# A four-layer graph network on one core: both halves of layer 0's rows in one step, and the last two output transfers moved to another queue

## The chip, the cores and the metric

The kernel runs on one core of a Trainium2 chip. The metric is the device time of one execution in microseconds, and smaller is better. A core has five engines with a queue each: TensorE (PE, matrix products; PEld is its weight load), VectorE (DVE), ScalarE (ACT), GpSimd (POOL) and SyncE (SP). Each works through its own queue in order. An instruction that has to wait holds everything behind it in that queue. SP and ACT also issue the DMA transfers here.

## The reference, cut to what matters

The input is `x` (4096 rows of 64) and a 0/1 matrix `adj` (4096 x 4096, float32, 67 MB). Four layers run one after the other, each as

```
x = layernorm(x + layer(x, adj, weights))
```

- Layer 0: `deg = sum of adj's row + 1`; `h = (adj @ x + x) / deg`; `z = relu([x, h] @ W + b)`; the result is `z / max(norm(z), 1e-12)` by rows.
- Layers 1 and 3 (hyperbolic attention): for each pair (i, j) a weight `sigmoid(left_i + right_j + b) * adj_ij` and a local vector `logmap(x_i, x_j)`; the weighted sum over j goes through `expmap` and a projection, which is row work: long chains of small operations on 8 numbers per partition.
- Layer 2: each row takes its last 100 neighbours with weights that halve from one to the next, times `x @ weight`, plus a bias.

## The kernel before, in words

**Tiling.** The 4096 rows of the result are four groups of 1024, in the order 3, 2, 1, 0 (`GROUPS`). A group has 8 blocks of 128 rows (`blocks(s)`). `adj` is read once in each layer for each group: 16 loads of 1 MB (`load`, L696 to L700), two blocks of 128 columns each, also from the last to the first. That makes 256 loads, all issued on SP, into six buffers (`f_loads`). A load can be issued only when its buffer is free again.

**Pairs and rows.** In every layer two kinds of work are interleaved. The *pairs* work through the loaded 1 MB pieces. In layer 0 (L1392 to L1440) they are eight bf16 products for each piece (L1408). In layers 1 and 3 (`attend`, L1025 to L1089) each block has six products into a `z` tile (L1059, L1062, L1065), a sigmoid and a square on ACT (L1074, L1077), two fused operations on DVE (L1080, L1082) and the products into `acc` (L1037). The *rows* are the work on a finished group: `end_0`, `norm_rows` and `prepare` after layer 0, `move` after layers 1 and 3. They are written as generators; each `yield n` asks to be continued n ticks later.

**What sets the order.** `later(steps, second)` puts a generator into one of two hand-made queues. `tick(n)` (L614 to L627), called by the pairs, continues the generator at the head of each of the two, queue 0 first. `near()` is 3 ticks in layer 0 and 1 in layers 1 to 3. Layer 0 has four ticks for each loaded piece. In layers 0 and 2 the order of the instructions of PE and ACT is the written order (`manual_schedule`); elsewhere, and on DVE, POOL and SP throughout, the compiler orders the ready instructions by its own estimates when the program is built. The order of each queue is then fixed.

**PSUM for row work.** Row work takes a PSUM buffer with `take` (L667 to L674). There is one, `aux`. While the list `spare` is not empty, a second is used in turn; in layer 0 it is `aux_2` (L1308 to L1310). `held` has an entry for each buffer taken; `free()` (L681 to L683) lets a step wait until `held` is empty, whichever queue it is in. `spare_ends()` (L676 to L679), called at the end of layer 0 (L1442), waits until `held` is empty and clears `spare`. The tiles of layer 1 (`p_sb`, L1446) are laid into the memory that layer 0's pools leave.

**`end_0` (L1357 to L1390)** makes the rows of a group from its sums, in two halves of four blocks. A half waits with `free()`, takes a buffer, makes eight pairs of float32 products (L1365, L1366), and takes them on DVE: a reciprocal of the degree (L1369), a multiplication (L1371) and the addition of `xw` (L1373). The first half ends with `yield near()`. Then come `relu` (L1376), the squares on POOL (L1378), the sum and root (L1380 to L1382), `norm_rows` and `prepare`. `prepare` queues its second part in queue 1: among other things four sets of transposes (L943) into a taken buffer, with a copy by ACT (L947). The last group's `end_0` is queued just before `spare_ends()`, so its steps run during the first ticks of layer 1.

**The end.** In layer 3 each group's new rows are written by `move` (L1098 to L1219) and sent out by `store` (L1611 to L1613), one transfer of 256 KB for each group, issued on ACT. `move` works on POOL for groups 3, 2 and 1 and on DVE for the last, group 0. It begins with two pairs of products (L1126), each copied by ACT (L1128). `attention` (L1452 to L1470) queues the store of a group while the next one's pairs run or behind them: the store of group 1 is queued when the pairs of group 0 are over, beside the `move` of group 0. After the stores the program reads a flag, `n_fit`, on every engine (L1652) and branches (L1653) over a general fallback that is not run here.

Of the kernel before, what the change touches and what calls it, by code (L numbers as in the profile page):

```python
# [10 lines left out]
F32 = mybir.dt.float32  # L11
# [8 lines left out]
P = 128  # L20
N = 4096
D = 64
# [3 lines left out]
SB = W // P  # L26
# [5 lines left out]
WB = WW // P  # L32
# [26 lines left out]
def gnn_stack_kernel(  # L59
# [15 lines left out]
    nc = tc.nc  # L75
    V = nc.vector
# [492 lines left out]
    def stream(fits):  # L569

        with ExitStack() as st:
# [19 lines left out]
            queues, place, done, held = ([], []), [0, 0], set(), []  # L591
# [65 lines left out]
            def near():  # L657

                return 3 if place[0] == 0 else 1
# [5 lines left out]
            spare, turn_of = [], [0]  # L665

            def take(dtype, *shape):  # L667


                held.append(1)  # L670
                turn_of[0] += 1
                if not spare or turn_of[0] % 2:
                    return aux.tile(list(shape), dtype, name="aux")
                return spare[0](dtype, shape)  # L674
# [6 lines left out]
            def free():  # L681
                while held:
                    yield 1  # L683
# [3 lines left out]
            def x_of(layer):  # L687

                if layer not in layers_x:
                    layers_x[layer] = xs.tile([P, NB, D], F32, name="x")  # L690
                return layers_x[layer]

            def blocks(s):
                return slice(s * WB, (s + 1) * WB)
# [7 lines left out]
            def grp(name, bufs=None):  # L702
                kw = {"bufs": bufs} if bufs else {}
                return row.tile([P, WB, D], F32, name=name, **kw)

            def nums(name, n=WB):
                return row.tile([P, n], F32, name=name)

            def over(v):
                return v[:, :, None].to_broadcast([P, v.shape[1], D])  # L710

            def rsqrt(a, name):

                n = a.shape[1]
                r, t = nums(name, n), nums("rs_t", n)
                V.tensor_scalar(
                    r.bitcast(I32), a.bitcast(I32), -0.5, float(0x5F3759DF), ALU.mult, ALU.add
                )
                for _ in range(3):
                    V.tensor_mul(t, r, r)  # L720
                    V.scalar_tensor_tensor(t, t, -0.5, a, ALU.mult, ALU.mult)
                    V.scalar_tensor_tensor(r, t, 1.5, r, ALU.add, ALU.mult)
                return r
# [138 lines left out]
            def norm_rows(layer, s, v, x2_to):  # L862

                m, v2, sq = nums("n_m"), nums("n_v2"), grp("sq")
                V.tensor_reduce(m, v, AX.X, ALU.add)
                V.tensor_scalar(m, m, 1.0 / D, None, ALU.mult)
                yield soon()
                V.tensor_sub(v, v, over(m))  # L868
                nc.gpsimd.tensor_mul(sq, v, v)  # L869
                yield soon()  # L870
                yield soon()
                V.tensor_reduce(v2, sq, AX.X, ALU.add)
                yield soon()
                V.tensor_scalar(m, v2, 1.0 / D, 1e-5, ALU.mult, ALU.add)
                r = rsqrt(m, "n_r")
                yield soon()
                V.tensor_mul(x_of(layer)[:, blocks(s), :], v, over(r))
                V.tensor_mul(x2_to, r, r)
                V.tensor_mul(x2_to, x2_to, v2)
                yield soon()  # L880
# [366 lines left out]
            def supports(s):  # L1247
# [40 lines left out]
                out=enter, in_=pass_by, compare_op=ALU.is_gt, fill=0.0, base=0,  # L1288
# [14 lines left out]
            with ExitStack() as lp:  # L1303
# [10 lines left out]
                xw = own.tile([P, NB, D], F32, name="xw")  # L1314
                sum_w = own.tile([P, D + 1], F32, name="sum_w")
                count_w = own.tile([D + 1, D + 1], F32, name="count_w")
# [39 lines left out]

                def end_0(s, tops):  # L1357
                    z = grp("z0")
                    for h, (top, low) in enumerate(tops):
                        yield from free()  # L1360
                        t = take(F32, P, SB, P)
                        for k in range(SB):
                            cols = slice(k * P, (k + 1) * P)
                            to = t[:, k, : D + 1]
                            nc.tensor.matmul(to, top[:, cols], sum_w, start=True, stop=False)  # L1365
                            nc.tensor.matmul(to, low[:, cols], count_w, start=False, stop=True)  # L1366
                        at = slice(s * WB + h * SB, s * WB + (h + 1) * SB)
                        d = nums("deg", SB)
                        V.reciprocal(d, t[:, :, D])  # L1369
                        zz = z[:, h * SB : (h + 1) * SB, :]  # L1370
                        V.tensor_mul(zz, t[:, :, :D], over(d))  # L1371
                        held.pop()
                        V.tensor_add(zz, zz, xw[:, at, :])  # L1373
                        if h == 0:
                            yield near()
                    V.tensor_scalar(z, z, 0.0, None, ALU.max)  # L1376
                    sq, n2 = grp("sq"), nums("n2")
                    nc.gpsimd.tensor_mul(sq, z, z)  # L1378
                    yield 1
                    V.tensor_reduce(n2, sq, AX.X, ALU.add)  # L1380
                    V.tensor_scalar(n2, n2, 1e-24, None, ALU.max)
                    n = rsqrt(n2, "n")  # L1382
                    yield 1
                    V.tensor_mul(z, z, over(n))
                    V.tensor_add(z, z, x0[:, blocks(s), :])
                    yield 1
                    yield from norm_rows(1, s, z, x2[:, blocks(s)])
                    yield from prepare(
                        1, s, att1, batt1_sb, curve1, 1e-15, good[:, 0], 70
                    )  # L1390

                with tc.manual_schedule(engines=FIXED):  # L1392
                    for s in GROUPS:
# [3 lines left out]
                        for g in reversed(range(NB // 2)):  # L1397
# [5 lines left out]
                            for k in (1, 0):  # L1403
                                j = 2 * g + k
                                for lhs, accs, m in parts:
                                    for h in range(2):
                                        at = k * WW + h * W
                                        nc.tensor.matmul(  # L1408
                                            accs[h][:m], lhs[:, j, :], edge[:, at : at + W],
                                            start=j == BLOCKS[0], stop=j == BLOCKS[-1],  # L1410
                                        )
                            if g == s * WB // 2 + 1:

                                for lhs, accs, m in parts:
                                    for h in range(2):
                                        for k in range(SB):
# [3 lines left out]
                                                start=False, stop=False,  # L1420
# [9 lines left out]
                        tops = []  # L1430
                        for h in range(2):
                            top = sb.tile([P, W], F32, name="top")
                            nc.scalar.copy(top, sums[h])
                            low = sb.tile([D + 1, W], F32, name="low")
                            nc.scalar.copy(low, counts[h][: D + 1])
                            tops.append((top, low))
                        later(end_0(s, tops))
                        if s > 0:
                            own_of = linear(0, s - 1, w0_sb[:D, :], own_part)
# [169 lines left out]
            place[0] = 3  # L1609

            def store(s):  # L1611
                nc.scalar.dma_start(out[:, blocks(s), :], x_of(4)[:, blocks(s), :])
                yield 1  # L1613

            attention(3, curve3, (4, 1, 1, 1), store)


            V.tensor_reduce(fits, odd, AX.X, ALU.add)
            V.tensor_scalar(fits, fits, 0.0, None, ALU.is_equal)
            t, g = nums("m1", 1), nums("g1", 1)  # L1620
# [26 lines left out]
    with tc.tile_pool(name="fit_ps", bufs=1, space=PSUM) as ps:  # L1647
        t = ps.tile([1, P], F32, name="fit_t")
# [52 lines left out]
```

## Time and profile before

| What | Value |
|---|---|
| Median of 3 runs (range) | 1115.99 us (1114.72 to 1119.29) |
| The profiled execution's own time | 1117.97 us |
| Its span, first to last instruction | 1116.2 us |
| Mean granted TensorE clock | 0.961 of full |
| Layer 0 and its seam, about | 0 to 200 us |
| Layers 1, 2 and 3, about | to 560, 800 and 1084 us |
| Last group's row work and end | 1084 to 1116.2 us |
| HBM read | 269.58 MB, 242 GB/s over the span |

How to read it. A line of the timeline gives the start in us, the duration in us, the engine, the line of the kernel, the operation, its output and input by name with shapes, and in brackets how long the engine was idle before it and what ended that idle time. ACTq and SPq are the sequencers of these engines; an issue of a DMA is such a line. A line of the chain gives start, duration, and what the time belonged to: the chain is followed back from the last instruction, at each step to what released it. A line of the windows gives a stretch of time, then for each of PE, PEld, DVE, ACT and POOL its busy us and, in brackets, how many instructions began in it, then the granted clock, the mean busy share of the 16 DMA engines and GB/s.

### The profile page before, as it was taken

What the parts mean: (1) busy time and instruction counts of PE and PEld (TensorE: products, weight loads), DVE (VectorE), ACT (ScalarE), POOL (GpSimd) and SP (SyncE); (2) the same over time, 40 slices, a digit from 0 to 9 for tenths busy, and PEclk for the clock granted to TensorE, in tenths of its full rate; (3) what the DMA queues carried; (4) which work ended last, traced back from release to release, by engine and by line L of the source; (5) the groups of instructions that cost most, each with busy time, mean ns of one, the idle gap of its engine ahead of it and who ended that gap; (6) DMA issues with size and microseconds to landing.
All of it is one profiled execution on the core that took longest, in us unless ns stands there. A gap on an engine that the chain in (4) does not pass through costs nothing.

```text
span 1116.2 us, 13744 instructions
## 1 busy us (share of the span) xinstructions
PE 996.4 (89%) x4861; PEld 393.9 (35%) x4949; DVE 912.1 (82%) x1452; ACT 803.4 (72%) x892; POOL 271.0 (24%) x649
## 2 busy tenths in 40 slices
PE   4998889789999999998998997788899999999960
PEld 2455455233333333332333332223333333333320
DVE  5677977999999999999366476447989999999965
ACT  0013122989999999896776788889899999998940
POOL 0011210010144443424500010000001544345281
PEclk8899999899999999999999999899899999999995
DMA  8899999546576576663987986587456766666300
GB/s 339 346 422 376 366 423 382 204 136 243 195 238 219 184 244 217 218 210 130 360 306 275 370 277 228 203 276 252 166 194 221 247 215 216 238 224 224 126 1 23
DMA packets 38581, 271.63 MB, mean 243 GB/s; under 512 B 4710, under 2 KB 4710, under 8 KB 5734
## 3 DMA queue, kind: packets, MB, share of 16 engines
q1 hardware_dynamic: 37440, 269.50, 66.4%
q10 hardware_dynamic: 1062, 1.15, 0.3%
q8 instruction: 41, 0.67, 0.2%
q14 instruction: 38, 0.31, 0.1%
HBM read 269.58 MB, written 1.05 MB: 242 GB/s over the span
## 4 chain that ended last, share of the span: by engine, by line
PE 58%; DVE 22%; ACT 9%; POOL 4%; DMA 4%; issue 3%; ACTq 0%; SPq 0%; POOLq 0%; DVEq 0%
PE acc L1037 14%; PE z L1563 9%; DVE t L1082 8%; DVE t L1080 6%; PE z L1062 6%; PE acc L1408 6%; PE z L1059 6%; PE z L1065 6%; PE acc L1575 3%; DMA edges<-in_adj_dram 3%; ACT sq L1077 3%; ACT sq L1570 3%; ACT sig L1074 2%; PE z L1575 1%; PE aux L943 1%
## 5 line engine op out<-in xcount | busy, mean ns | idle before, releaser
L1080 DVE SCALAR_TENSOR_TENSOR t<-z,sig 128x1024 f32<-128x1024 f32 x256 | 308.9, 1218 | 13.8 <-ACT sq L1077 7.7
L1077 ACT ACTIVATE sq<-z,turn 128x1024 f32<-128x1024 f32 x256 | 278.1, 1112 | 46.2 <-PE z L1065 17.8
L1082 DVE SCALAR_TENSOR_TENSOR t<-sq,t 128x2048 f32<-128x2048 f32 x128 | 297.4, 2323 | 0.5
L1074 ACT ACTIVATE sig<-left_b,right 128x1024 f32<-128x1024 f32 x256 | 286.2, 1147 | 1.8 <-DVE t L1080 1.3
L1037 PE MATMUL acc<-t,xe 128*64 128x512 f32 x1024 | 255.6, 611 | 18.4 <-DVE t L1082 17.9
L1062 PE MATMUL z<-lo_hi,hi_lo 128*128 128x512 f16 x512 | 194.6, 380 | 3.8 <-issue 1.0
L1065 PE MATMUL z<-dst,src 74*128 74x512 f16 x512 | 195.6, 382 | 0.0
L1059 PE MATMUL z<-edges,two_i 128*128 128x512 bf16 x462 | 181.5, 393 | 8.1 <-DVE t L1080 8.1
L1570 ACT ACTIVATE sq<-z,at_edge 128x512 bf16<-128x512 f32 (+1 forms) x192 | 149.4, 829 | 44.4 <-PE z L1563 41.3
L838 DVE SCALAR_TENSOR_TENSOR t<-edges 128x2048 bf16<-128x2048 f32 x32 | 73.0, 2288 | 52.8 <-DMA edges<-in_adj_dram 52.8
L1037 PEld LDWEIGHTS acc<-t,xe 128*64 128x64 f32 x1024 | 63.8, 137 | 147.5 <-issue 83.6
L1563 PE MATMUL z<-edges,pass_by 128*128 128x512 bf16 x241 | 87.6, 400 | 18.4 <-ACT sq L1570 17.6
L1059 PEld LDWEIGHTS <-two_i 128*128 128x128 bf16 x512 | 50.2, 98 | 127.5 <-issue 82.8
L1408 PE MATMUL acc<-edges,first 128*128 128x512 bf16 x241 | 78.0, 400 | 16.1 <-DMA edges<-in_adj_dram 15.5
L1563 PE MATMUL z<-edges,enter 128*128 128x512 bf16 x240 | 85.0, 397 | 0.5
L1408 PE MATMUL acc<-edges,third 128*65 128x512 bf16 x256 | 81.4, 400 | 0.9 <-issue 0.4
L838 DVE SCALAR_TENSOR_TENSOR junk<-edges 128x2048 bf16<-128x2048 f32 x32 | 73.1, 2286 | 4.6 <-DMA edges<-in_adj_dram 4.3
L1065 PEld LDWEIGHTS <-src 74*128 74x128 f16 x512 | 49.3, 96 | 70.5 <-issue 8.4
L1062 PEld LDWEIGHTS <-hi_lo 128*128 128x128 f16 x512 | 50.4, 98 | 58.0 <-issue 12.5
L1575 PE MATMUL acc<-sq,halves 128*64 128x512 bf16 x384 | 61.6, 398 | 2.6 <-issue 1.6
L869 POOL TENSOR_TENSOR sq<-z 128x512 f32<-128x512 f32 x8 | 14.1, 1759 | 162.2 <-DVE z L868 139.5
L1133 POOL TENSOR_TENSOR w_att<-x,u 128x512 f32<-128x512 f32 x6 | 15.6, 2599 | 142.9 <-ACT u L1128 142.9
(375 smaller groups left out, 939.4 us busy)
## 6 DMA issues: line engine op xcount, KB each, us to landing
edges<-in_adj_dram SPq DMA_DIRECT2D x256, 1024.0 KB, 5.0
x<-in_x_dram SPq DMA_DIRECT2D x4, 256.0 KB
out_dram<-x ACTq DMA_DIRECT2D x4, 256.0 KB
w_sb<-in_L_gnn_W_dram ACTq DMA_DIRECT2D x1, 32.0 KB, 5.9
w_twice<-in_L_gnn_weight_dram ACTq DMA_DIRECT2D x2, 16.0 KB, 8.2
given<-in_L_gnn_b_dram ACTq DMA_DIRECT2D x1, 0.2 KB
given<-in_L_gnn_bias_dram ACTq DMA_DIRECT2D x1, 0.2 KB
given<-in_L_gnn_b_att_dram ACTq DMA_DIRECT2D x1, 0.0 KB
```

The costliest lines, as they stand in the source:

```text
L838: V.scalar_tensor_tensor(junk, a, 0.0, a, ALU.not_equal, ALU.not_equal, accum_out=odd[:, n : n + 1])
L1037: it = nc.tensor.matmul(acc[h * D : (h + 1) * D, :], xe[:, j, :], t[:, k, h * W : (h + 1) * W], start=j == BLOCKS[0], stop=j == BLOCKS[-1],)
L1059: nc.tensor.matmul(half, two_i, edge[:, at : at + W], start=True, stop=False)
L1062: nc.tensor.matmul(half, hi_lo[:, of], lo_hi[:, to], start=False, stop=False)
L1065: last = nc.tensor.matmul(half, src[:, of], dst[:, to], start=False, stop=True)
L1074: nc.scalar.activation(sig, left_b, AF.Sigmoid, bias=right[:, j : j + 1])
L1077: nc.scalar.activation(sq[:, k], zp, AF.Square, bias=turn, scale=-1.0 / UNIT)
L1080: V.scalar_tensor_tensor(t[:, k], zp, 0.0, sig, ALU.max, ALU.mult)
L1082: V.scalar_tensor_tensor(t, sq, HIGH**2, t, ALU.add, ALU.mult)
L1408: nc.tensor.matmul(accs[h][:m], lhs[:, j, :], edge[:, at : at + W], start=j == BLOCKS[0], stop=j == BLOCKS[-1],)
L1563: nc.tensor.matmul(z[:, h : h + W], lhs, rhs[:, h : h + W], start=j == BLOCKS[0], stop=True, skip_group_check=True,)
L1570: nc.scalar.activation(w, z[:, :n], AF.Exp, bias=at_edge, scale=-LN2)
```

## The change

It has two parts. In `end_0`, one `free()` stands ahead of both halves. Where `spare` is not empty, the products of both halves are made first, into two buffers, and then both are taken on DVE, with no tick between. Where it is empty, the halves go one after the other with `yield near()` between them as before, but `held` keeps its entries until both are taken, so that no other step gets a buffer in between. In `store`, the transfers of groups 1 and 0 are issued on SP and those of groups 3 and 2 on ACT as before.

```diff
--- before.py
+++ after.py
@@ -1356,23 +1356,29 @@
 
                 def end_0(s, tops):
                     z = grp("z0")
-                    for h, (top, low) in enumerate(tops):
-                        yield from free()
-                        t = take(F32, P, SB, P)
-                        for k in range(SB):
-                            cols = slice(k * P, (k + 1) * P)
-                            to = t[:, k, : D + 1]
-                            nc.tensor.matmul(to, top[:, cols], sum_w, start=True, stop=False)
-                            nc.tensor.matmul(to, low[:, cols], count_w, start=False, stop=True)
-                        at = slice(s * WB + h * SB, s * WB + (h + 1) * SB)
-                        d = nums("deg", SB)
-                        V.reciprocal(d, t[:, :, D])
-                        zz = z[:, h * SB : (h + 1) * SB, :]
-                        V.tensor_mul(zz, t[:, :, :D], over(d))
-                        held.pop()
-                        V.tensor_add(zz, zz, xw[:, at, :])
-                        if h == 0:
+                    yield from free()
+
+                    for some in ((0, 1),) if spare else ((0,), (1,)):
+                        ts = []
+                        for h in some:
+                            top, low = tops[h]
+                            t = take(F32, P, SB, P)
+                            for k in range(SB):
+                                cols = slice(k * P, (k + 1) * P)
+                                to = t[:, k, : D + 1]
+                                nc.tensor.matmul(to, top[:, cols], sum_w, start=True, stop=False)
+                                nc.tensor.matmul(to, low[:, cols], count_w, start=False, stop=True)
+                            ts.append((h, t))
+                        for h, t in ts:
+                            at = slice(s * WB + h * SB, s * WB + (h + 1) * SB)
+                            d = nums("deg", SB)
+                            V.reciprocal(d, t[:, :, D])
+                            zz = z[:, h * SB : (h + 1) * SB, :]
+                            V.tensor_mul(zz, t[:, :, :D], over(d))
+                            V.tensor_add(zz, zz, xw[:, at, :])
+                        if some == (0,):
                             yield near()
+                    held.clear()
                     V.tensor_scalar(z, z, 0.0, None, ALU.max)
                     sq, n2 = grp("sq"), nums("n2")
                     nc.gpsimd.tensor_mul(sq, z, z)
@@ -1609,7 +1615,9 @@
             place[0] = 3
 
             def store(s):
-                nc.scalar.dma_start(out[:, blocks(s), :], x_of(4)[:, blocks(s), :])
+
+                queue = nc.sync if s <= 1 else nc.scalar
+                queue.dma_start(out[:, blocks(s), :], x_of(4)[:, blocks(s), :])
                 yield 1
 
             attention(3, curve3, (4, 1, 1, 1), store)
```

## The prediction

> **What bounds the kernel now.** I read the page first (busy shares and the summary of the chain), then the chain in order of time over its two ends that the change touches, then the ACT timeline there, then all engines at the seam between layer 0 and layer 1, and last the windows of layer 0.
>
> The page: no engine is the bound throughout.
>
> ```profile
> PE 996.4 (89%) x4861; PEld 393.9 (35%) x4949; DVE 912.1 (82%) x1452; ACT 803.4 (72%) x892; POOL 271.0 (24%) x649
> PE 58%; DVE 22%; ACT 9%; POOL 4%; DMA 4%; issue 3%; ACTq 0%; SPq 0%; POOLq 0%; DVEq 0%
> ```
>
> The reader is to see POOL with 4% of the chain though it is the idlest engine, so somewhere the end waits for it. The ACT timeline of the last 33 us shows where:
>
> ```profile
> 1083.04 0.59 ACT L1088 COPY sums<-acc 128x512 f32<-128x512 f32 x1 [9.56 <-PE acc L1037]
> 1092.12 0.34 ACTq L1612 DMA_DIRECT2D out_dram<-x  x1
> 1092.50 0.38 ACT L1128 COPY ys<-aux 128x260 f32<-128x260 f32 x1 [8.88 <-POOL x L1218]
> 1094.26 0.38 ACT L1128 COPY ys<-aux 128x260 f32<-128x260 f32 x1 [1.38 <-PE aux L1126]
> 1094.67 0.63 ACT L1134 ACTIVATE xw<-ys 128x512 f32<-128x512 f32 x1
> 1100.79 0.21 ACT L1164 ACTIVATE th<-un 128x8 f32<-128x8 f32 x1 [5.49 <-DVE un L1158]
> 1111.58 0.34 ACTq L1612 DMA_DIRECT2D out_dram<-x  x1
> ```
>
> The store of group 1 (1092.12) stands on ACT's queue ahead of the first copy of the last group's `move`. The store needs group 1's rows from POOL; the copy (L1128) needs only four PE products that ran at 1083.68 for 0.71 us. ACT stood 8.88 us. The chain confirms that this wait decides the end:
>
> ```profile
> 1090.91 1.19 POOL x L1218
> 1092.12 0.34 ACTq L1612
> 1092.50 0.39 ACT ys L1128
> 1092.93 1.25 PE aux L1126 x4
> 1094.26 0.39 ACT ys L1128
> ```
>
> The other place is the seam, where layer 1's first tiles lie in the memory that layer 0 leaves:
>
> ```profile
> 188.97 0.18 DVE L1369 RECIPROCAL deg<-aux 128x4 f32<-128x4 f32 x1 [1.92 <-PE aux L1366]
> 191.22 1.06 PE L943 MATMUL aux<-ident,ys 128*128 128x128 f16 x8
> 192.31 1.01 ACT L947 COPY lo_hi<-aux 128x1024 f16<-128x1024 f16 x1 [4.24 <-PE aux L943]
> 195.44 0.18 DVE L1369 RECIPROCAL deg<-aux 128x4 f32<-128x4 f32 x1 [5.37 <-PE aux L1366]
> 196.69 1.28 ACT L1074 ACT_TABLE_LOAD   x1 [3.37 <-DVE z L1373]
> 203.03 0.59 PE L1059 MATMUL z<-edges,two_i 128*128 128x512 bf16 x1 [5.77 <-DVE t L1080]
> ```
>
> Group 0's halves are taken at 188.97 and 195.44. Between them the single aux buffer went to group 1's `lo_hi` transposes. The first sigmoid (ACT L1074) waited 3.37 us for the second half's last add (L1373, done 196.53), and PE then stood 5.77 us. Layer 0 itself runs at the transfers' rate (columns: PE, PEld, DVE, ACT, POOL busy; clock; DMA share; GB/s):
>
> ```profile
> 70.00:83.00 13.00, 12.90 (x77) 7.49 (x79) 10.82 (x34) 0.58 (x1) 2.95 (x1) 1.00 1.01 421
> 83.00:96.00 13.00, 10.35 (x45) 4.61 (x45) 12.83 (x42) 1.66 (x3) 2.86 (x7) 1.00 0.86 321
> ```
>
> **What the Trainium skill says.** "DMA: Bandwidth & Descriptors", Anatomy of one DMA: DMA engines do not wait on semaphores; the wait is held by the issuing sequencer before dispatch. The trace agrees: 8.88 us. The same page, Issuing engines are not separate DMA queues: a transfer runs on the same 16 engines whichever engine issues it. The trace agrees as to the issue: 327 to 328 ns on SP (L698), 338 to 377 on ACT (L1612). "GPSIMD Engine Reference", Specifications: GpSimd shares its SBUF interfaces with VectorE and contends with instructions with two SBUF inputs. The trace agrees: POOL's L1218 takes 1.18 us in the tail with DVE idle, 3.11 at most beside DVE. "TensorE: Matmul & The Clock Gate", Part 1: the clock falls to half after an idle window. The trace agrees: a granted 0.52 and 0.50 in 199 to 205 us, where PE stood.
>
> **The change, part by part.** *Stores on SP.* The copy can start as soon as its products are there: 1083.68 + 0.71 = 1084.39, and 0.1 for the hand-over (1094.16 to 1094.26 at the second copy), so 1084.49 instead of 1092.50: **-8.0 us**. From there to 1111.58 all is one chain of the last group (copy, PE, copy, DVE), which shifts whole. POOL's work on group 1 (1084.6 to 1092.1) now lies beside it. A DVE product of this size beside POOL took 1.08 (L1133 at 570.99) against 0.69 alone: +0.4. The smaller steps (0.17 each) may stretch over some 3.3 us while POOL runs its three wide ones; the least is 0, the most a doubling, +1.6. I take +0.3 for both: **-7.7**, bounds -8.0 and -6.0. POOL's own chain, stretched by its ratio 3.11/1.18 on its three wide operations (3.3 us in all), adds at most 5.4 us and ends at 1097.5; the last group ends near 1103.6, so group 1's store does not become the end.
>
> What SP's wait holds up: the last of the 256 loads (L698) was issued at 1043.2, so no load is behind it. Behind it are the last store and the read of n_fit (0.47 + 0.19 + 0.03 + 0.05 us: load, register operations, assertion, branch). Before, SP did these at 1096.8 in the shade; now they follow the last store. Their cover is that store's landing: issued until 1111.92, the next semaphore step on DVE at 1114.7, so 2.8 us against some 0.9. Cost 0; without the cover +1.0. The issue moves from 0.34 on ACT to 0.33 on SP: 0. Stores of groups 3 and 2 (938.2, 1028.8) stay.
>
> *Both halves of layer 0's rows.* The number of instructions is the same: 8 times 16 products, 8 reciprocals, 8 multiplications, 8 additions. What goes is one waiting step of three ticks and a wait for a free buffer in each group. For groups 3, 2 and 1 a second buffer stands in `spare`, so both halves go out together; their later row steps move up by three or four ticks, about one pair of blocks, 2.7 us (43 us for 16). Does the stage gain? It moves bytes at a share near 1.0 in most windows, so an earlier row step only changes where the dips lie (0.86 in 83 to 96). The five dips to 0.86, 0.90, 0.94, 0.98 and 0.93 of 13 us each are worth 5.1 us together: if half vanish, -2.5; if half as much is added, +2.5. I take **0**, since moving does not remove DVE work that delays the checks (L838), which free buffers.
>
> Group 0 is different: `spare` is emptied before its rows are made, so it still goes one half at a time, but the buffer is no longer offered to the other queue between the halves. The second half needs only aux back from DVE: 189.18 + 0.42 = 189.60. If PE takes it at once, it starts at 189.7 instead of 193.4: -3.7. If it stands behind the six products of the first z, it starts when `lo_hi` did, 191.2: -2.2; part of that is given back while PE's clock is low there (0.62 in 190 to 193). If PE's order puts it behind both z, nothing is gained: 0. What is late next is the row chain L1376 to L1384, which shifts with it, and the table load of 1.28. I take **-2.0**, bounds -4.0 (some of the half clock gone too) and 0. It carries to the end because PE, DVE and ACT alternate on the chain through layers 1 to 3, with no DMA wait of weight after layer 0.
>
> Sum: -7.7 - 2.0 + 0 = -9.7. The profiled execution took 1117.97 (span 1116.2, 1.8 around it), so 1108.3 on its own scale. It is 2.0 over the median of the runs, 1115.99; on that scale the forecast is **1106.3**.
>
> **Rivals.** (A, likeliest) both as above: 1106.3, its own range 1104 to 1107.5. (B) The row part gives nothing, because PE's order keeps the second half behind both z, or a later wait takes it back; only the tail counts: 1108.3. For it: the order is fixed at build from estimates, and three of four groups are DMA-bound. Against: the wait for L1373 is plain in the trace. (C) The seam gives its full 4 and layer 0's dips half vanish: 1115.99 - 7.7 - 4 - 2.5 = 1101.8. (D) The tail's wait is replaced: group 1's few DVE steps, or POOL beside DVE, hold the last group, and 5 of the 8 return: 1106.3 + 5 = 1111.3. For it: one DVE step (L754 at 1084.82) still stands between; against: it is done before the copy would be. (E, other side) In layer 0 the row steps, now one pair earlier, go ahead of the DVE checks, edge buffers come free later and loads are issued later. The gain of 9.7 turns into a loss of 0.5% when layer 0 loses over 15.3 us: its 130 us of windows at a mean share near 0.97 would have to fall to about 0.86, each as bad as the worst now. With 17 us lost: 1123. Against: six edge buffers, and no row work is added. That the change does not do what it says holds in part, for group 0, and is counted.
>
> **How the numbers follow.** Chances: A 0.45, B 0.25, C 0.14, D 0.11, E 0.05. About 0.5% (5.6 us) is what a measurement of this kernel can tell from no change: faster means under 1110.4. A, B and C lie there whole, D mostly in "same": faster 0.85, same 0.10, slower 0.05. The range takes in A, B, C with the bounds of the unknown costs (-8.0 - 4.0 - 2.5 = -14.5, 1101.5, less 1.3 for the spread under the median, 1100) and reaches to D (1112).
>
> **What would show it.** In the tail: ACT's first L1128 of ys within 2 us of L1088, no store ahead of it, both late stores on SP, the last one near 8 us earlier after the last L1037. At the seam: the second L1369 within 4 us of the first, no L943 between, ACT's wait for L1373 shorter. In layer 0: the windows' DMA shares about as now. Wrong if the copy still waits for POOL, if DVE's steps in the tail are stretched by several us, or if layer 0 ends later than 187 us.

## The result and the profile after

| | Before | After |
|---|---|---|
| Median (range) of 13 runs each | 1113.92 us (1110.21 to 1119.29) | 1107.84 us (1104.74 to 1113.9) |
| Profiled execution, its own time | 1117.97 us | 1108.28 us |
| Its span; mean granted clock | 1116.2 us; 0.961 | 1106.6 us; 0.966 |

The ratio after to before is 0.995, with a 95% interval of 0.9933 to 0.9967. Times 1113.92 that is -5.6 us (-7.5 to -3.7): faster, with an interval clear of no change, but by 0.5% only. The forecast of 1106.3 was -9.7 from its median of 1115.99, so the direction was right and 4.1 us did not come. In absolute time the forecast lies only 1.5 us from the measured 1107.84, and that is luck: the median of the first 3 runs of before was 2.1 us above that of all 13, which hides half of what did not come. The two profiled executions differ by 9.7 us, which happens to equal the forecast; the table of stages below shows that this is a coincidence.

The ACT timeline of the end, after:

```profile
1078.44 0.58 ACT L1088 COPY sums<-acc 128x512 f32<-128x512 f32 x1 [8.02 <-PE acc L1037]
1079.83 0.38 ACT L1128 COPY ys<-aux 128x260 f32<-128x260 f32 x1 [0.80 <-PE aux L1126]
...
1090.38 0.21 ACT L1164 ACTIVATE th<-un 128x8 f32<-128x8 f32 x1 [8.28 <-DVE un L1158]
```

No store stands ahead of the first copy. It comes 1.39 us after L1088 (9.46 before) and waits only for its products. The chain's summary on the page has POOL at 3% instead of 4%. But ACT's next wait, for the DVE chain that ends in L1158, has grown from 5.49 to 8.28 us. The timeline of all engines shows what DVE did meanwhile, first one step of that chain in before, then after:

```profile
1098.45 0.17 DVE L759 TENSOR_TENSOR rs_t<-r_t 128x8 f32<-128x8 f32 x1
```

```profile
1086.08 1.04 POOL L1214 TENSOR_TENSOR w_att<-x,p 128x512 f32<-128x512 f32 x1
1086.21 0.92 DVE L759 TENSOR_TENSOR rs_t<-r_t 128x8 f32<-128x8 f32 x1
1087.08 1.04 POOL L1215 TENSOR_TENSOR u<-u,q 128x512 f32<-128x512 f32 x1
1087.17 0.97 DVE L739 SCALAR_TENSOR_TENSOR rs_t<-rs_t,t 128x8 f32<-128x8 f32 x1
...
1088.19 1.19 POOL L1218 TENSOR_TENSOR x<-u,w_att 128x512 f32<-128x512 f32 x1
1088.37 1.03 DVE L759 TENSOR_TENSOR rs_t<-r_t 128x8 f32<-128x8 f32 x1
1089.41 12.10 SPq L1620 DMA_DIRECT2D out_dram<-x  x2
```

Each of POOL's three wide products on group 1 catches one small step of the last group on DVE. Alone such a step takes 0.17 us; here it starts 0.1 to 0.2 us after the product and ends with it. The excess is 0.75 + 0.80 + 0.86 = 2.4 us. POOL's wide products take 1.04, 1.04 and 1.19, as before (1.04, 1.05, 1.18), so they lose nothing. The order of the starts matters: at 1081.97, where DVE's wide L1133 had begun 0.17 us ahead, it was a small POOL step (L759) that took 0.57 us instead of 0.20. The last line is both stores, grouped: group 1's at 1089.41, the last one at 1101.16.

At the seam, timeline of all engines after:

```profile
180.70 0.59 ACT L1439 COPY top<-acc 128x512 f32<-128x512 f32 x1
...
183.63 0.18 DVE L1375 RECIPROCAL deg<-aux 128x4 f32<-128x4 f32 x1
184.41 0.56 PE L1369 MATMUL aux<-sum_w,top 128*128 128x65 f32 x2 [0.82 <-DVE z L1377]
...
189.33 0.18 DVE L1375 RECIPROCAL deg<-aux 128x4 f32<-128x4 f32 x1 [4.61 <-PE aux L1370]
190.59 1.28 ACT L1074 ACT_TABLE_LOAD   x1 [6.95 <-DVE z L1378]
196.93 0.59 PE L1059 MATMUL z<-edges,two_i 128*128 128x512 bf16 x1 [4.45 <-DVE t L1080]
```

The second half comes 5.7 us after the first instead of 6.5, with no transposes (L943) between. Its first two products go out at 184.41, then the six products of the first `z` stand in between, until 187.33. PE's stall before the next `z` is 4.45 us instead of 5.77. The first line is ACT's copy of group 0's sums in layer 0. It comes 41.8 us after that of group 1 (138.89); in before it came 44.5 us after it (141.57):

```profile
186.03 0.59 ACT L1433 COPY top<-acc 128x512 f32<-128x512 f32 x1
```

So 2.7 us of the seam's gain are there before group 0's rows begin. Layer 0 itself, in the same two windows as in the prediction:

```profile
70.00:83.00 13.00, 12.56 (x72) 6.49 (x71) 11.46 (x28) 0.00 (x0) 2.95 (x1) 1.00 1.00 416
83.00:96.00 13.00, 10.11 (x55) 4.87 (x55) 12.76 (x41) 3.78 (x6) 2.72 (x7) 1.00 0.84 330
```

The DMA share is 1.00 and 0.84, against 1.01 and 0.86.

**Stages compared.** Single spans can't be compared here: the start, up to the sums of group 3, differs by several us between executions of the same code. So I cut each profile at the same instructions and list the stretches in us. "Sums 0" is from ACT's copy of group 1's sums in layer 0 to its copy of group 0's. "Seam" is from the same copy of group 1's sums to the first L1080 of layer 1, and so contains "sums 0". "To S1" is from the same copy to the end of layer 1's first group (its L1088), and so contains the seam. "Layer 2" is from layer 1's last L1088 to layer 3's first. "Last pairs" is from the last but one L1088 to the last, "tail" from there to the issue of the last store, "end" from there to the end of the span.

| Kernel | start | sums 0 | seam | to S1 | layer 2 | last pairs | tail | end | span |
|---|---|---|---|---|---|---|---|---|---|
| before | 56.6 | 44.46 | 60.19 | 150.06 | 327.27 | 76.37 | 28.54 | 4.66 | 1116.2 |
| before, again | 54.1 | 45.42 | 61.15 | 151.23 | 325.89 | 74.82 | 30.05 | 4.87 | 1112.9 |
| after | 54.3 | 41.80 | 56.77 | 150.05 | 326.90 | 74.81 | 22.72 | 5.39 | 1106.6 |
| after, again | 52.9 | 43.55 | 59.14 | 150.26 | 325.89 | 74.81 | 22.74 | 5.37 | 1104.8 |
| stores only | 49.9 | 47.01 | 61.15 | 150.89 | 327.20 | 76.33 | 22.46 | 5.35 | 1104.2 |
| rows only | 54.6 | 43.49 | 56.81 | 150.03 | 329.30 | 74.83 | 30.02 | 4.54 | 1116.7 |
| store of group 1 only | 52.9 | 46.99 | 61.12 | 150.85 | 327.19 | 76.33 | 22.48 | 4.50 | 1106.3 |
| rows, store of group 1 | 53.6 | 44.20 | 57.53 | 151.98 | 327.02 | 74.81 | 22.75 | 4.68 | 1107.5 |

The stretches left out (layer 0 between groups 3 and 1, the rest of layer 1, the second and third group of layer 3) lie within 84.2 to 85.0, 235.5 to 236.4 and 152.2 us in all eight. The 9.7 us between the first profiles of before and after are -2.3 in the start, -1.6 in the last pairs, -5.8 in the tail, +0.7 at the end and -0.7 elsewhere. The first two are not shown to be the change's: the same code repeated gives another start, and before repeated has 74.82 in the last pairs as well.

### The profile page after: what moved, and what is told of

Read it like the earlier page. It is cut to its first block, busy times and chain, and to the rows that moved or that the text cites. A ratio compares the mean times of both kernels' runs of the same rounds, so it can differ in the third digit from the quotient of the medians.

```text
span 1106.6 us, 13832 instructions
## 1 busy us (share of the span) xinstructions
PE 1001.9 (91%) x4949; PEld 392.4 (35%) x4949; DVE 915.5 (83%) x1452; ACT 803.1 (73%) x892; POOL 273.1 (25%) x649
## 3 DMA queue, kind: packets, MB, share of 16 engines
HBM read 269.58 MB, written 1.05 MB: 245 GB/s over the span
## 4 chain that ended last, share of the span: by engine, by line
PE 55%; DVE 24%; ACT 9%; DMA 5%; POOL 3%; issue 2%; ACTq 0%; SPq 0%; POOLq 0%; DVEq 0%
PE acc L1037 15%; PE z L1569 9%; DVE t L1082 7%; PE z L1059 7%; PE z L1065 6%; PE z L1062 6%; DVE t L1080 6%; DMA edges<-in_adj_dram 4%; PE acc L1581 3%; PE acc L1414 3%; ACT sq L1077 3%; ACT sq L1576 2%; DVE junk L838 2%; ACT sig L1074 1%; PE z L1581 1%
## 5 line engine op out<-in xcount | busy, mean ns | idle before, releaser
L1080 DVE SCALAR_TENSOR_TENSOR t<-z,sig 128x1024 f32<-128x1024 f32 x256 | 308.8, 1217 | 13.0 <-ACT sq L1077 6.8
L1082 DVE SCALAR_TENSOR_TENSOR t<-sq,t 128x2048 f32<-128x2048 f32 x128 | 297.3, 2322 | 0.5
L1037 PE MATMUL acc<-t,xe 128*64 128x512 f32 x1024 | 255.2, 608 | 17.2 <-DVE t L1082 16.8
L1059 PE MATMUL z<-edges,two_i 128*128 128x512 bf16 x512 | 201.2, 393 | 7.4 <-DVE t L1080 7.4
L1037 PEld LDWEIGHTS acc<-t,xe 128*64 128x64 f32 x1024 | 63.8, 136 | 145.6 <-issue 83.8
L1569 PE MATMUL z<-edges,enter 128*128 128x512 bf16 x256 | 91.0, 398 | 0.0
L869 POOL TENSOR_TENSOR sq<-z 128x512 f32<-128x512 f32 x8 | 14.2, 1776 | 164.3 <-DVE z L868 132.2
L1133 POOL TENSOR_TENSOR w_att<-x,u 128x512 f32<-128x512 f32 x6 | 15.6, 2595 | 141.2 <-ACT u L1128 141.2
```

Source lines behind the costliest of these rows:

```text
L1037: it = nc.tensor.matmul(acc[h * D : (h + 1) * D, :], xe[:, j, :], t[:, k, h * W : (h + 1) * W], start=j == BLOCKS[0], stop=j == BLOCKS[-1],)
L1059: nc.tensor.matmul(half, two_i, edge[:, at : at + W], start=True, stop=False)
L1080: V.scalar_tensor_tensor(t[:, k], zp, 0.0, sig, ALU.max, ALU.mult)
L1082: V.scalar_tensor_tensor(t, sq, HIGH**2, t, ALU.add, ALU.mult)
L1569: nc.tensor.matmul(z[:, h : h + W], lhs, rhs[:, h : h + W], start=j == BLOCKS[0], stop=True, skip_group_check=True,)
```

## The experiments

**Stores only**: the second part of the change alone.

```diff
-                nc.scalar.dma_start(out[:, blocks(s), :], x_of(4)[:, blocks(s), :])
+                queue = nc.sync if s <= 1 else nc.scalar
+                queue.dma_start(out[:, blocks(s), :], x_of(4)[:, blocks(s), :])
```

> The rows of layer 0 as before, only the last two stores on SP. Theory 1 (the stores bring all of the measured 5.6 us, and the tail's gain was cut from 8.0 to about 5 by three DVE steps that POOL's wide products hold up and by 0.8 at the very end): about 5 us faster, ratio 0.9955, from the copy of the last sums (L1088) to the issue of the last store 22.7 us instead of 28.5, three small DVE steps of 0.9 to 1.0 us. Theory 2 (the stores bring what was forecast, and the rows cost): 7.7 us faster, ratio 0.993. Theory 3 (the rows bring a part that lasts): 3 us faster, ratio 0.9973.

Measured: 1106.22 us (6 runs) against 1114.91, ratio 0.9923 (0.9894 to 0.9953). The tail is 22.46, the end 5.35. Three small DVE steps are long here too, at other places of the chain (L1148 0.97, L1149 0.97, L759 1.02), each under one wide product. So it is not a property of one operation or one tile, and what counts is what DVE has next when POOL starts.

**Rows only**: the first part alone, `end_0` as in the change and the stores on ACT.

> Only the rows of layer 0 changed, all stores on ACT. Theory 1: no change, ratio 0.999 to 1.001; the first DVE operation of layer 1 (L1080) comes up to 1 us sooner after the copy of group 0's sums, and this is lost again by the end of layer 1's first group; ACT still stands 8.9 us behind group 1's store. Theory 2: 2 us slower, ratio 1.002. Theory 3: 2.6 us faster, ratio 0.9977.

Measured: 1114.31 us (22 runs) against 1114.91, ratio 0.9997 (0.9981 to 1.0012). The rows bring nothing that 22 runs can show, at most 2.1 us. Yet the profile has the seam at 56.81, 3.4 shorter than before. ACT's end in this kernel:

```profile
1092.73 0.34 ACTq L1618 DMA_DIRECT2D out_dram<-x  x1
1093.11 0.38 ACT L1128 COPY ys<-aux 128x260 f32<-128x260 f32 x1 [10.35 <-POOL x L1218]
```

The last L1088 came 1.5 us earlier after the one before than in the first profile of before (74.83 for 76.37), and ACT then waited 1.5 us longer for POOL (10.35 for 8.88). Last pairs and tail together are 104.85 and 104.91: with the store on ACT, POOL sets the end, and a gain just ahead of it is lost.

**Store of group 1 only**: before, with one store moved.

```diff
-                nc.scalar.dma_start(out[:, blocks(s), :], x_of(4)[:, blocks(s), :])
+                queue = nc.sync if s == 1 else nc.scalar
+                queue.dma_start(out[:, blocks(s), :], x_of(4)[:, blocks(s), :])
```

> Rows as before; only group 1's store on SP, the last one stays on ACT. Theory 1: all of the tail's gain is in group 1's store: at least as fast as with both on SP. If the 0.8 us longer end (from the last store's issue to the end of the span 5.4 instead of 4.6) comes from SP having to issue the store and then close the program, it is 4.6 here and the kernel is 5.8 us faster than before; if it is scatter of the transfer's landing, 5.0 us faster, as with both.

Measured: 1106.81 us (7 runs), ratio 0.993 (0.9905 to 0.9956). The tail is the same as with both stores (22.48), the end is 4.50 instead of 5.35. Group 1's store has the whole gain; in these profiles moving the last one costs 0.85 at the end.

**One wide product more on POOL**: after, with L1214 done twice for group 1 in layer 3 (the repeat changes no value).

```diff
                 E.tensor_mul(w, xg, over(p))
+                if layer == 3 and s == 1:
+                    E.tensor_mul(w, xg, over(p))
```

> The changed kernel with one of group 1's three wide products on POOL in layer 3 (L1214) made twice; the output stays the same. Theory 1 (a DVE step with two inputs that meets a wide POOL product waits until that product ends): a fourth small DVE step of 0.9 to 1.0 us instead of 0.17, and from L1088 to the last store's issue 23.6 us instead of 22.7. Rival (the three long steps come from something else, such as the store's issue or a semaphore): three long steps as before, 22.7 us.

Measured: tail 23.54 against 22.72, one run (1106.97 us). Timeline of all engines in this kernel:

```profile
1085.98 1.03 POOL L1216 TENSOR_TENSOR w_att<-x,p 128x512 f32<-128x512 f32 x1
1086.07 0.97 DVE L739 SCALAR_TENSOR_TENSOR r_t<-rs_t,r_t 128x8 f32<-128x8 f32 x1
```

The product that was added catches a fourth step, 0.97 - 0.17 = 0.80, and the tail grows by 0.82. This is a dose test: one wide product more, one small step more that is held to its end.

**Rows and the store of group 1**: after, with the last store back on ACT (`s == 1` in place of `s <= 1`).

> The rows of layer 0 as changed, group 1's store on SP, the last store on ACT. If what the profiles so far show adds up (tail 28.5 to 22.6 us, end 4.6 to 4.5, rows 0 to 0.9 to the end of layer 1's first group, and 1.5 more if PE's clock stays full for the last eight products as it did in all three kernels with the changed rows): 6.0 to 8.5 us faster than before, ratio 0.9925 to 0.9945, and 0.8 faster than the change as it was. If the full clock there is chance and not the rows' doing, the time from the copy of group 1's sums to that of group 0's in layer 3 is 76.3 us here and not 74.8.

Measured: 1109.3 us (22 runs) against 1115.23, ratio 0.9944 (0.9927 to 0.996). The end is 4.68 instead of 5.39, as with the store of group 1 only. Against the before of the same round that is -6.2 us, for -5.6 with both stores on SP: the expected direction, but less apart than either can tell.

**Group 0's rows only, and the other groups' rows only**: before, with the new body of `end_0` under `if s == 0:`, or under `if s > 0:`, and the old one under `else:`.

> Before, with the changed rows for group 0 alone (no buffer offered to the other queue between its halves), groups 3, 2 and 1 as before. If the seam's gain comes from this part, the first L1080 of layer 1 comes 56.8 to 58 us after the copy of group 1's sums in layer 0 (before 60.2 to 61.2, all rows changed 56.8 to 57.2). If it comes from the earlier rows of the other groups, which let group 1's transposes of lo_hi go ahead of the seam, it stays at 60 to 61. Either way the first group of layer 1 ends 150.0 to 150.9 us after that copy, if the gain is given back there.

> The other part alone: changed rows for groups 3, 2 and 1, group 0 as before. If group 0's part makes the seam's gain: the first L1080 60 to 61 us after the copy of group 1's sums in layer 0. If the others' earlier steps make it: 56.8 to 58. The copies of layer 0's own groups 3 to 1 lie 84.3 to 85 us apart as in every run so far, since the stage is bound by transfers.

Measured, one run each: with group 0's rows alone 1121.27 us, sums 0 45.50, seam 61.95, to S1 155.06; with the others alone 1114.54 us, sums 0 44.11, seam 60.86, to S1 150.55. Neither part alone brings the seam below before's 60.2 to 61.2. With group 0's alone both halves and the first `z` ran at half clock (0.50 granted from 190 to 198 us) and ACT waited 9.35 us for them. With the others alone group 0's sums come early, but transposes (now those of `src`) stand between the halves again, which are 7.5 us apart. So in these two runs the gain at the seam needs both, and group 0's part alone seems to cost some 5 us by S1.

**A wide product on ACT**: the kernel of the last but one experiment (rows and the store of group 1), with L1214 for group 1 in layer 3 made by ACT in eight pieces.

```diff
-                E.tensor_mul(w, xg, over(p))
+                if layer == 3 and s == 1:
+                    for i in range(WB):
+                        nc.scalar.mul(w[:, i, :], xg[:, i, :], p[:, i : i + 1])
+                else:
+                    E.tensor_mul(w, xg, over(p))
```

> As e5, and one of group 1's three wide products in layer 3 (L1214) goes from POOL to ACT, in eight pieces; the output stays the same. If wide POOL products hold up DVE steps one for one: two long DVE steps instead of three, and from L1088 to the last store's issue 21.7 us instead of 22.5. If ACT's pieces delay the tanh of the last group (L1164) that stands on the same queue, up to 1 us of it is lost again.

Measured: 1113.32 us, one run. No DVE step is long, and from the second L1128 to L1164 the chain takes 6.53 us, as in before, for 9.32 in after. But the last pairs end at 82.55 instead of 74.81. ACT's timeline of this kernel:

```profile
1085.42 0.59 ACT L1216 ACTIVATE w_att<-x,p 128x64 f32<-128x64 f32 x2 [15.23 <-POOL p L743]
1085.92 0.56 ACT L1088 COPY sums<-acc 128x512 f32<-128x512 f32 x1
```

The pieces were put on ACT's queue ahead of the last group's sums (L1088) and wait for POOL's `p`. The stall that the change took away is back in another form, and 7.7 us are lost. As a cure it fails, but it shows the chain's time with no POOL product beside it, and a second time what a waiting instruction on ACT's queue costs.

**The square of layer 1's first `norm_rows` on ACT** instead of POOL, in the kernel with the rows and the store of group 1. In after, the DVE step L975 at 204.14 takes 1.05 us instead of 0.16, under a POOL product of `norm_rows`; the question was whether this eats the seam's gain.

```diff
-                nc.gpsimd.tensor_mul(sq, v, v)
+                if layer == 1 and s == 0:
+                    nc.scalar.activation(sq, v, AF.Square)
+                else:
+                    nc.gpsimd.tensor_mul(sq, v, v)
```

> As e5, and the squares of group 0's rows in layer 0's norm (L869) made by ACT instead of POOL; the output stays the same. In every kernel with all rows changed this POOL product (1.04 us) met a small DVE product at the seam (L975: 1.05 us instead of 0.16), which took back 0.9 of the seam's gain. If POOL's product is the cause, L975 is back at 0.16 us and the second L1082 of layer 1 comes 0.5 to 0.9 us sooner after the first than the 8.1 us of the changed kernel. If L975 is long for another reason, it stays at 1.05.

Measured: the step takes 0.17, the second L1082 comes 6.8 us after the first instead of 8.1, but the stretch to S1 is 150.33 us. That is less than in the one profile of the kernel that it was made from (151.98), and no less than in after, rows only and the kernel with one more product (150.03 to 150.26), whose layers 0 and 1 are the same. One run, 1109.34 us. The shorter distance shows little, since the first L1082 itself came late (seam 59.53): the second stands 69.82 us after group 1's sums, 69.90 in after repeated, where L975 is held, and 68.31 in after. The held step was real; that it decides is not shown.

**Before and after, profiled again**, unchanged, to see what the profiles show by chance.

> The kernel before once more, for PE's clock at the end: its last eight products (L1037) took 3.48 us at half clock, as in the two kernels with the rows of before, and 1.94 us in all six with changed rows, with the same instructions ahead of them. If the kernel decides this, 3.4 to 3.5 us again, and 76.3 us from the copy of group 1's sums to that of group 0's. If chance does, either value.

> The changed kernel once more, for the same question: 1.94 us for the last eight products and 74.8 us between the copies if the kernel decides it, either value if chance does. And the tail again: 22.7 us from L1088 to the last store's issue, with three long DVE steps, and 5.3 to 5.4 us from there to the end of the span.

Measured: 1114.63 and 1106.49 us; the stages are in the table. Tail, end and to S1 repeat within 0.3 in after. The seam moved from 56.77 to 59.14 while to S1 stayed. In before, last pairs and tail moved by 1.5 in opposite directions. PE's last eight products of group 0 in before, repeated:

```profile
1076.01 1.94 PE L1037 MATMUL acc<-t,xe 128*64 128x512 f32 x8 [2.79 <-DVE t L1082]
```

In after they take 1.94 too; in the first profile of before the same eight, after an idle time of 2.80, took 3.48. The granted clock was 0.54 during the 3.48 us, 1.00 during the 1.94. The same code has both values, so the rows alone don't decide the 1.5 us. That they shift the odds is not excluded: all four profiles of the table with changed rows have 74.8 in the last pairs, and three of the four without have 76.3 or 76.4.

## Why the prediction was right, and where it was not

**The stall on ACT (-8.0): right.** The first copy stands 1.39 us after L1088 instead of 9.46, which is -8.07. The copy needed nothing else, and the store of group 1 on SP held nothing up.

**"+0.3" for POOL beside DVE, bounds 0 to +1.6: the term that was mis-sized.** It measured +2.4. The mechanism, group 1's wide products lying beside the last group's chain, was named, but its size was taken from a slow-down (0.69 to 1.08, "a doubling"). What the trace shows is a hold: the small step ends only with the product, so here the price was 0.75 to 0.86 for each wide product that a step met. The Trainium skill says this in "SBUF — State Buffer", Who interferes with whom, which the prediction did not use: "Whoever issues first gets the shared pair for the whole instruction; the other fully blocks", and a DVE instruction with two SBUF inputs contends with a GpSimd instruction that reads SBUF. The trace agrees for L759 and L739. In the kernel with the stores only a `TENSOR_SCALAR` with one tensor as input was held too (L1149, 0.97); the same section lists `tensor_scalar` among the operations that can contend. The runs show the hold; that a shared port is behind it is the page's statement. The 3.11 us of L1218, which the prediction read as a stretching of POOL by 3.11/1.18, was such a hold in before's own trace:

```profile
368.15 1.04 POOL L1215 TENSOR_TENSOR u<-u,q 128x512 f32<-128x512 f32 x1
368.24 3.09 DVE L1082 SCALAR_TENSOR_TENSOR t<-sq,t 128x2048 f32<-128x2048 f32 x1
369.27 3.11 POOL L1218 TENSOR_TENSOR x<-u,w_att 128x512 f32<-128x512 f32 x1
```

DVE's L1082 (2.28 us alone) begins under L1215 and takes 0.8 more; L1218 begins under L1082, and ends 1.05 us after it, which is about its time alone. With the three wide products of before's tail (L1214, L1215, L1218 at 1088.79 to 1092.09) a price near 2.4 could have been worked out from that. The tail then closes: 28.54 - 8.07 + 2.4, less 0.5 because the second four products of L1126 ran at full clock (0.71 us at a granted 1.00, for 1.25 at 0.50), plus 0.3 because DVE took group 1's L754 (1081.72) ahead of the last group's L1133, is 22.7; measured 22.72. So the tail gave -5.8, not -7.7. The -0.5 and the +0.3 were not foreseen and nearly cancel. Rival D had named this family, with 5 of the 8 returning; 2.2 did.

**"POOL's own chain stretched by up to 5.4": did not happen.** POOL's wide products started first and kept their time. Its chain from L754 to the store's issue took 7.69 us for 7.30; the 0.4 are L759, held under L1133.

**The read of n_fit, cost 0, without cover +1.0: wrong in place, and the end was mis-sized.** On SP the read stands between the two stores (1089.8), not behind the last, so it costs nothing. But the end grew all the same. SP's and DVE's closing semaphore steps in before, and then in after:

```profile
L1653 SPq EVENT_SEMAPHORE  x8: 17/17/17, 1100.4 to 1114.9; - x8
...
L1653 DVEq EVENT_SEMAPHORE  x1: 21/21/21, 1114.7 to 1114.7; - x1
```

```profile
L1661 SPq EVENT_SEMAPHORE  x8: 17/17/17, 1104.7 to 1105.2; - x8
...
L1661 DVEq EVENT_SEMAPHORE  x1: 21/21/21, 1104.5 to 1104.5; - x1
```

In before SP had done some of its eight steps long ahead of DVE's last; in after all eight follow it. The end is 5.35 to 5.39 in the four profiles with the last store on SP and 4.50 to 4.87 in the nine with it on ACT: +0.7. Of that, between the first profiles, 0.2 lie ahead of DVE's closing step (3.36 us after the issue, for 3.12) and 0.5 behind it. That the 0.5 are SP's steps fits the trace and was not tried by itself.

**Layer 0's stage 0: right up to group 1's sums, wrong behind them.** Between groups 3 and 1 it takes 84.2 to 85.0 in all kernels of the table. But from group 1's sums to group 0's it takes 41.8 to 44.2 us in all eight profiles with the rows of groups 3, 2 and 1 changed, and 44.5 to 47.0 in the five without (with group 0's rows alone 45.5). Why is open.

**The seam -2.0, "It carries to the end": the step that failed.** The seam did get shorter, if all groups are changed: 56.8 to 57.5 us in three profiles of the table and 59.1 in the repeat, for 60.2 to 61.2 without. But it is for the most part another gain than the one that was forecast. Between the first profiles the first L1080 comes 3.4 us sooner, and 2.7 of these are the earlier sums of group 0, in the stage that was put at 0. The part that the prediction counted, the second half behind the first, is 0.2 to 0.8 us: the halves are 5.7, 6.3, 4.1 and 4.1 us apart in the four profiles of the table with changed rows, for 6.5, 6.5, 4.9 and 4.9 in those without (two levels occur with either code, and like is set beside like). ACT's wait for the last addition was to be shorter and is longer (6.95 for 3.37), since the copy of `lo_hi` (L947) that stood between the halves at 192.31 is done ahead of both, at 182.61 (as with the rows of groups 3, 2 and 1 alone). That the seam gained the forecast 2.0 and more is therefore luck. And the gain does not carry: to S1 are 150.05 and 150.26 us in after against 150.06 and 151.23 in before and 150.89 and 150.85 with the stores alone. L1082 on DVE shows where it goes. In after, with group 1's sums at 138.89:

```profile
199.12 2.28 DVE L1082 SCALAR_TENSOR_TENSOR t<-sq,t 128x2048 f32<-128x2048 f32 x1
...
255.11 2.28 DVE L1082 SCALAR_TENSOR_TENSOR t<-sq,t 128x2048 f32<-128x2048 f32 x1
```

With stores only, where they are at 134.30, the first and the tenth as well:

```profile
198.91 2.28 DVE L1082 SCALAR_TENSOR_TENSOR t<-sq,t 128x2048 f32<-128x2048 f32 x1
...
251.41 2.28 DVE L1082 SCALAR_TENSOR_TENSOR t<-sq,t 128x2048 f32<-128x2048 f32 x1
```

Counted from those sums, after leads by 64.61 - 60.23 = 4.4 us at the first and by 117.11 - 116.22 = 0.9 at the tenth (against the first profile of before by 3.4 and 0.05). Of the 3.5 given back, 1.6 go between the first and the second L1082 (where the held L975 stands; 0.8 in after repeated), the others between the seventh (235.69 in after) and the tenth, beside and behind the transposes of group 0's `prepare`. Six products L1037 take 2.83 us there (at 237.29) and 1.93 with stores only (at 233.93), at a granted clock of 0.67 and 1.00; that is 0.9 us of it. Without the held step the stretch to S1 was no shorter, so what fixes the 150 us to S1 stays open. A likely reason, argued and not shown, is that group 0's row work, which layer 1's pairs carry with them, ends at its own time.

**The sum.** Tail -5.8, end +0.7, rows 0 within what can be told: -5.1, against -5.6 (-7.5 to -3.7) measured. The -7.8 and -8.6 of the two kernels with stores alone are medians of 7 and 6 runs; their intervals reach to -4.9 and -5.2, so the runs don't show that the rows cost anything. Of the rivals, B (rows give nothing, 1108.3) is the nearest to the measured 1107.84 in absolute time. As differences from before the forecasts are -9.7 (A), -7.7 (B), -14.2 (C) and -4.7 (D), and only D lies within the measured interval. What happened is B's rows with part of D's contention in the tail, so no single one was right. No version is clearly ahead of the change; the smallest edit, one store on SP, has all of the gain that can be measured.

## What to carry to other kernels

A DMA that waits for another engine's result belongs on a queue with nothing urgent behind it; look for it as a short issue line on a compute engine with a long idle time after it. When the stall goes, list the wide GpSimd operations that will then lie beside a chain of small VectorE steps, and charge each one at most its whole length less one small step (here 0.75 to 0.86 of 1.04 to 1.19 us). A gain at a seam counts only from a later fixed point that both kernels pass: measure to the end of the next stage before adding it to the sum.

## What the runs showed of the hardware that was not expected

- A VectorE step of 128x8 (0.17 us alone) was held 0.90 to 1.03 us under a GpSimd product of 128x512 that had begun ahead of it; the GpSimd product kept its 1.04 (1.19 for the last). Four products held four steps, three held three. It works the other way too: a GpSimd step of 128x8 took 0.57 instead of 0.20 under a VectorE product of 128x512 that had begun ahead of it.
- The issue of the last output transfer from SP instead of ACT made the time from that issue to the end of the span 0.7 us longer (5.35 to 5.39 for 4.50 to 4.87).
- Eight identical products after an idle time of 2.8 us took 1.94 or 3.48 us in executions of the same code, at a granted clock of 1.00 and 0.54.
- The same code's layer 2 took 325.9 or 327.3 us in before and 326.9 or 325.9 in after, and the start up to group 3's sums 56.6, 54.1 and 49.9 in three profiles whose code is the same there (before twice, stores only): with spreads like these, stages read at fixed instructions tell more than spans.
